# A recurrence whose small matrix products stand in two groups a step instead of three

## The chip, the core and the metric

The kernel runs on one core of a Trainium2 chip. The core has five engines with a queue of their own each: TensorE (PE in the profile, with its weight loads as PEld), VectorE (DVE), ScalarE (ACT), GpSimd (POOL) and SyncE (SP), which only issues transfers here. An engine takes its queue in order; an instruction that waits for a semaphore holds up what is queued behind it. Matrix products read SBUF and write PSUM. The metric is the time of one execution on the device, in microseconds.

## The reference

Two transformer layers in float32. The first layer, which the change touches, adds three things: its input, a gated feed-forward (hidden 512, inner 1408) and a "TTT" attention, in which a small weight matrix is trained while the sequence is read. Batch 4, 512 tokens, 32 heads of width 16, in 32 steps of 16 tokens:

```python
def step(carry, x):
    W1_s, b1_s = carry
    xq, xk, xv, eta_mb = x
    Z1 = xk @ W1_s + b1_s
    grad = _ln_fused_l2_bwd(Z1, xv - xk, ln_w, ln_b)
    Attn1 = jnp.tril(xq @ xk.swapaxes(-1, -2))
    b1_bar = b1_s - jnp.tril(eta_mb) @ grad
    Z1_bar = xq @ W1_s - eta_mb * Attn1 @ grad + b1_bar
    W1_new = W1_s - (last_eta * xk).swapaxes(-1, -2) @ grad
    b1_new = b1_s - jnp.sum(last_eta * grad, axis=-2, keepdims=True)
    out = xq + _ln(Z1_bar, ln_w, ln_b)
    return ((W1_new, b1_new), out)
```

The outputs are normalised over 512 and projected. The second layer (latent attention and a group of experts) follows and is not changed.

## The kernel before, in words

Everything is in one function, `trunk_kernel`, that records instructions for all engines. The recording layer then puts each engine's instructions in an order of its own: an instruction whose data are early can be placed ahead of earlier ones. An instruction that is handed to `tc.keep_in_program_order` is held in the program's order on its engine. The resulting order of each engine is fixed when the program is built; it can be read from the built program ("the built order").

**The recurrence** (loop at L781) has 32 steps, n = 0 to 31. A state of 128 (b, head) blocks lives in the PSUM tile wacc. A step has these parts:

- `weights_out` (L328): the state is copied from wacc into the block-diagonal operand wq_bd (L332: two copies on DVE, two on ACT) and, masked for two heads, into wh (L335, ACT).
- `first_product` (L338): one full product with bones, and 16 **quarter products** pz (128 rows by 32 columns of the array, so that four stand side by side): keys times state, and keys times queries, from sk and wq_bd.
- `queries_out` (L410): 16 quarter products, queries times state, from wh and wq_bd into the PSUM tile pso (the *query product*).
- `gradient` (L353): a chain of small operations, nearly all on DVE (L356 to L390), to grad.
- `out_operands` (L418): grad is masked for two heads into gh on POOL (L421) and the attention part of pz into a_bd on DVE (L424).
- `update` (L393): four copies of grad into the block-diagonal g_bd (L395, DVE and ACT), then 16 quarter products from km and g_bd into wacc (the *update*), and gsum on DVE.
- `emit_out` (L434): 16 quarter products from gh and a_bd into pso, on top of the query product (the *output product*); then DVE adds the bias into zch (L449) and updates bias_o (L450). After the fourth step of a chunk, POOL stores zch to DRAM (z, L454) and loads it back in another layout (zb, L456).
- `prepare` (L303) for the next step, on POOL: the load of kv (L307), sk (L314), four copies of the queries into the other columns of wq_bd (L316), km (L321).

**The work beside it.** The feed-forward, the projections and the finishing of earlier chunks (`finish`, L545: squares pn_sq, a full product with bones, reciprocals, and more) are generators, each of whose pieces carries a cost in microseconds; `fill(us)` (L702) records pieces until their costs add up to what is due. The step calls it three times with the entries of GAPS, 11, 3 and 8 us (10, 3 and 7 in the last chunk): between output operands and update, between update and output product, and behind the output product. Their products are full ones (128 rows by 128 columns), 256 or 512 columns long: pf (gate and up), pd (down), pj (projections, transposes, finishing). A float32 product shows as two passes in the trace. The loads of their weights (wg, wu, wd) are issued by SP.

All quarter products are recorded through one helper, `mm` (L116, L117), so they all carry line L117 in the profile and are told apart by their tiles.

Of the kernel before, what the change touches and what calls it, by code (L numbers as in the profile page):

```python
# [23 lines left out]
NH, HD, K = 32, 16, 16  # L24
NM = L // K
# [30 lines left out]
def trunk_kernel(ctx: ExitStack, tc: tile.TileContext, a: dict, out: bass.AP):  # L56
    nc = tc.nc
# [48 lines left out]
    with ExitStack() as px:  # L106
# [7 lines left out]
        quarters = [slice(32 * q, 32 * q + 32) for q in range(4)]  # L114

        def mm(out, lhsT, rhs, start=True, stop=True):  # L116
            nc.tensor.matmul(out, lhsT=lhsT, rhs=rhs, start=start, stop=stop, skip_group_check=True)  # L117

        def psum():
            return ps_pj.tile([P, 512], F32, tag="pj", name="pj")  # L120
# [48 lines left out]
        def by_head(name):  # L169

            return a[name].rearrange("(al r) (be bp h d) -> al r be bp h d", al=4, be=4, bp=2, h=2)[:, 0, :, 0]
# [4 lines left out]
        for name in ("gamma", "beta"):  # L176
            nc.scalar.dma_start(
                out=row[name].rearrange("o (be al x) -> o be al x", be=NC, al=4),
# [13 lines left out]
        def spread_row(dst, src):  # L192
            pr = psum()[:, : src.shape[-1]]
            mm(pr, one_row, src)
            nc.vector.tensor_copy(dst, pr)
# [10 lines left out]
        for h in range(2):  # L206
            r = slice(4 * h, 4 * h + 4)
            nc.gpsimd.dma_start(
                out=sel8[r], in_=a["bones"].rearrange("(be h r) p -> h be r p", be=4, h=2)[h, :, 0]
# [32 lines left out]
        def features(ch, w, got, tag, bufs):  # L242

            t = got[ch] = wk.tile([P, NC, CW], F32, tag=tag, name=f"{tag}_{ch}", bufs=bufs)
            for be in range(NC):
                pp = psum()[:, :CW]
                for c in range(NC):
                    mm(pp, w[:, c, be * P : (be + 1) * P], xTs[ch][:, c, :], c == 0, c == NC - 1)
                nc.scalar.copy(t[:, be, :], pp)
                yield 1.72  # L250
# [49 lines left out]
        def spread(ap):  # L300
            return ap.unsqueeze(2).to_broadcast([P, NG, HD])
# [26 lines left out]
        def weights_out(n):  # L328

            flat = wacc.rearrange("p b be d -> p (b be) d")  # L330
            for al, r in enumerate(quarters):
                (nc.vector.tensor_copy if al < 2 else nc.scalar.copy)(wq_bd[r, :, al, :HD], flat[r])  # L332
            wh = wk.tile([P, NG, 2, HD], F32, tag="wh", name=f"wh_{n}")
            for h in range(2):
                nc.scalar.mul(wh[:, :, h, :], flat, m2[:, h : h + 1])  # L335
            return wh.rearrange("p g h d -> p g (h d)")

        def first_product(n, pre):  # L338

            pz = ps_st.tile([P, NG, 2 * HD], F32, tag="pz", name=f"pz_{n}")  # L340
            mm(pz[:, :, :HD], bones, gsum.rearrange("p b al d -> p (b al) d"), True, False)
            for b in range(B):
                for be, r in enumerate(quarters):
                    mm(
                        pz[r, 4 * b : 4 * b + 4, :],
                        pre["sk"][:, 4 * b + be, :],
                        wq_bd[:, 4 * b + be],
                        False,
                        True,
                    )  # L350
            return pz
# [41 lines left out]
        def update(n, g, pre):  # L393
            for be, r in enumerate(quarters):
                (nc.vector.tensor_copy if be < 2 else nc.scalar.copy)(g_bd[r, :, be, :], g[r])  # L395
            for b in range(B):
                for al, r in enumerate(quarters):
                    mm(
                        wacc[r, b].rearrange("p be d -> p (be d)"),
                        pre["km"][:, 4 * b + al, :],  # L400
                        g_bd[:, 4 * b + al].rearrange("p be d -> p (be d)"),
                        False,
                        True,
                    )
            flat = gsum.rearrange("p b al d -> p (b al) d")
            nc.vector.scalar_tensor_tensor(flat, g, ntok, flat, ALU.mult, ALU.add)
# [3 lines left out]
        def queries_out(n, wh):  # L410

            po = ps_st.tile([P, NC, 4, K + 1], F32, tag="pso", name=f"pso_{n}")
            for be in range(NC):
                for b, r in enumerate(quarters):
                    mm(po[r, be, :, :K], wh[:, 4 * b + be, :], wq_bd[:, 4 * b + be, :, HD:], be == 0, False)
            return po

        def out_operands(n, g, pz):  # L418
            gh = wk.tile([P, NG, 2, HD], F32, tag="gh", name=f"gh_{n}")
            for h in range(2):  # L420
                nc.gpsimd.tensor_scalar_mul(gh[:, :, h, :], g, m2[:, h : h + 1])  # L421

            for be, r in enumerate(quarters):
                nc.vector.scalar_tensor_tensor(  # L424
                    a_bd[r, :, be, :K],
                    pz[r, :, HD:],
                    1.0,
                    mneg[r].unsqueeze(1).to_broadcast([32, NG, K]),
                    ALU.add,
                    ALU.mult,  # L430
                )
            return gh

        def emit_out(n, po, gh):  # L434

            ch, i = divmod(n, CH)
            for al in range(4):
                for b, r in enumerate(quarters):
                    mm(
                        po[r, :, al, :],  # L440
                        gh[:, 4 * b + al].rearrange("p h d -> p (h d)"),
                        a_bd[:, 4 * b + al],
                        False,
                        True,
                    )
            if i == 0:
                zch[ch] = wk.tile([P, NG, CT], F32, tag="zch", name=f"zch_{ch}", bufs=1)
            flat = po.rearrange("p be al t -> p (be al) t")
            nc.vector.tensor_add(zch[ch][:, :, i * K : (i + 1) * K], flat[:, :, :K], spread(bias_o))  # L449
            nc.vector.tensor_add(bias_o, bias_o, flat[:, :, K])  # L450
            if i == CH - 1:
                dst = z_d[ch].rearrange("(x hd) b t -> hd x b t", hd=32)
                for b, r in enumerate(quarters):
                    nc.gpsimd.dma_start(out=dst[:, :, b, :], in_=zch[ch][r])  # L454
                zbs[ch] = wk.tile([P, NC, CW], F32, tag="zb", name=f"zb_{ch}", bufs=1)
                nc.gpsimd.dma_start(out=zbs[ch], in_=z_d[ch].rearrange("(be p) b t -> p be (b t)", p=P))  # L456
# [45 lines left out]
        for j, name in enumerate(("gamma", "beta")):  # L502
            nc.gpsimd.dma_start(
                out=ch8[4 * j : 4 * j + 4], in_=by_head(name).rearrange("al be h d -> be al (h d)")
# [197 lines left out]
        def fill(us):  # L702
            nonlocal due
            due += us
            while due > 0 and (v := next(work, None)) is not None:
                due -= v
# [39 lines left out]
        def zeroed(name, shape):  # L746
            t = one.tile(shape, F32, tag=name, name=name)
            nc.gpsimd.memset(t, 0.0)
            return t


        wq_bd = zeroed("wq_bd", [P, NG, 4, 2 * HD])
# [28 lines left out]
        for n in range(NM):  # L781
            wh = weights_out(n)
            pz = first_product(n, pre)
            po = queries_out(n, wh)
            g = gradient(n, pz, pre)
            gh = out_operands(n, g, pz)

            gaps = GAPS if n // CH + 1 < NCHUNK else LAST_GAPS
            fill(gaps[0])
            update(n, g, pre)  # L790
            fill(gaps[1])
            emit_out(n, po, gh)
            fill(gaps[2])
            if n + 1 < NM:
                while (n + 1) // CH not in done:
                    fill(1.0)
                pre = prepare(n + 1)
# [111 lines left out]
    with ExitStack() as px:  # L909
# [197 lines left out]
        for e in range(E):  # L1107
            if e == 1:
# [9 lines left out]
                for t, rows in ((cos, slice(0, HALF)), (sin, slice(HALF, RD))):  # L1118
                    for k in range(E):
                        nc.sync.dma_start(  # L1120
                            out=t[:HALF].rearrange("p (k e j) -> p k e j", k=NCHUNK, e=E)[:, :, k],
# [10 lines left out]
            if e == 2:  # L1132

                pb = psp.tile([P, 2, E, NHG], F32, tag="pa", name="pb")
                for j, wr in enumerate((wkr, wqr)):
                    by_head = b_raw[:, j].rearrange("p (hg h) -> p h hg", h=HPG)
                    for m in range(E):
                        t = ident[:, m:RD:2] if m < 2 else wr[:, HALF * (m - 2) : HALF * (m - 1)]
                        for h, r in enumerate(quarters):
                            nc.tensor.matmul(  # L1140
                                pb[r, j, m],
                                lhsT=t,
                                rhs=by_head[:, h],
                                start=True,
                                stop=True,
                                skip_group_check=True,
# [18 lines left out]
    with ExitStack() as px:  # L1165
# [227 lines left out]
        for u, (hg, b) in enumerate(units):  # L1393
# [15 lines left out]
            for i in range(E):  # L1409
                n = E * u + i  # L1410
# [121 lines left out]
```

## Time and profile before

| | |
|---|---|
| three runs | 2002.38, 2007.29, 2008.54 us; median 2007.29 |
| profiled execution | 2001.78 us, span 2000.0 us |
| the 32 steps | 47.3 us (first product of step 0) to 903 us |
| PE busy / POOL busy | 1939.4 us / 515.9 us |
| 128x32 quarter products, 16 a step of each kind | pz 0.276 us a pass, query 0.219, update 0.222, output 0.225 (their lengths overlap) |

The busy share of an engine is that of its instructions' modelled lengths. Quarter products are issued so that they overlap, so distances between starts say more than lengths. A wait ("idle before ... <- releaser") is the time in which an engine did nothing, put down to what released it. PEclk is the share of its full clock that TensorE was granted.

### The profile page before, as it was taken

To read this page: it belongs to the slowest core of one execution; us is meant where nothing else is said; L and a number is where in the kernel's file an instruction comes from. 1 tells how busy PE (TensorE), PEld (TensorE's weight loads), DVE (VectorE), ACT (ScalarE), POOL (GpSimd) and SP (SyncE) were. 2 spreads that over 40 slices of the span, in tenths; PEclk is the share of its full clock that TensorE was granted. 3 is DMA by queue.
4 is the path that set the end of the run, shared out by engine and by line. 5 is a ranking of instruction groups with operands and counts; after the bars stand their busy time and mean duration, and the time that the engine had idled before them with its cause. 6 is when DMAs were issued, how large, how long until landed. Compare 5 with 4: busy or idle time off the path is not lost.

```text
span 2000.0 us, 32373 instructions
## 1 busy us (share of the span) xinstructions
PE 1939.4 (97%) x11626; PEld 1233.0 (62%) x11626; DVE 1170.9 (59%) x2579; ACT 815.8 (41%) x1695; POOL 515.9 (26%) x619
## 2 busy tenths in 40 slices
PE   8999999999999999998999999999999999999997
PEld 6777676767767676743777745555555555555555
DVE  5445757475666566574555566555655556555664
ACT  2224334334334342432222165554554455445552
POOL 4334343424243343412000101111211121322110
PEclk9999999999999999999999999999999999999999
DMA  6657566646465455746652144444444434333343
GB/s 167 199 138 212 143 188 169 181 115 192 123 172 167 124 175 152 229 117 200 224 167 63 44 112 127 123 102 109 105 103 107 106 102 112 93 97 97 102 107 103
DMA packets 227307, 273.50 MB, mean 137 GB/s; under 512 B 88587, under 2 KB 117452, under 8 KB 226508
## 3 DMA queue, kind: packets, MB, share of 16 engines
q1 hardware_dynamic: 206656, 239.28, 43.5%
q0 software_dynamic: 8992, 26.84, 4.7%
q10 hardware_dynamic: 11500, 5.32, 0.9%
q8 instruction: 93, 1.52, 0.3%
q14 instruction: 66, 0.54, 0.1%
HBM read 174.18 MB, written 34.87 MB: 105 GB/s over the span
## 4 chain that ended last, share of the span: by engine, by line
PE 49%; DVE 1%; DMA 1%; SPq 0%; ACT 0%; issue 0%; DVEq 0%; ACTq 0%
PE pc L1254 11%; PE sc L1207 9%; PE pq L1184 8%; PE px L1301 5%; PE p L1301 4%; PE pk L1184 3%; PE epg L976 3%; PE epo L1039 1%; PE epu L976 1%; PE eox L1069 1%; PE pvo L891 1%; PE pw L866 1%; PE eo L1069 1%; DMA gu<-in_gu 0%; SPq L1246 0%
## 5 line engine op out<-in xcount | busy, mean ns | idle before, releaser
L1225 DVE TENSOR_REDUCE st<-sc 128x1 f32<-128x512 f32 x256 | 168.9, 681 | 242.4 <-PE sc L1207 242.4
L1227 ACT ACTIVATE prob<-sc,st 128x512 f32<-128x512 f32 x256 | 175.1, 686 | 213.7 <-DVE st L1225 213.5
L1254 PE MATMUL pc<-prT,lv 128*128 128x512 f32 x512 | 232.5, 597 | 5.2 <-DMA out<-y 3.9
L1236 DVE STREAM_TRANSPOSE tt<-prob 128x512 f32<-128x512 f32 x256 | 178.4, 700 | 46.6 <-ACT prob L1232 37.1
L1232 ACT ACTIVATE prob<-prob,st 128x512 f32<-128x512 f32 x256 | 182.0, 720 | 58.2 <-DVE st L1231 58.2
L117 PE MATMUL pf<-xT,wg 128*128 128x256 f32 x704 | 174.7, 390 | 4.1 <-DMA wg<-in_wg 2.7
L1184 PE MATMUL pq<-cq,uq 128*128 128x512 f32 x384 | 175.2, 592 | 0.0
L117 PE MATMUL pf<-xT,wu 128*128 128x256 f32 x704 | 168.2, 382 | 0.9 <-DMA wu<-in_wu 0.7
L117 PE MATMUL pd<-wd,hid 128*128 128x512 f32 x352 | 166.3, 601 | 1.3 <-DMA wd<-in_wd 1.3
L1254 PEld LDWEIGHTS pc<-prT,lv 128*128 128x128 f32 x512 | 96.8, 191 | 106.8 <-issue 104.5
L117 PEld LDWEIGHTS pf<-xT,wg 128*128 128x128 f32 x704 | 133.1, 193 | 31.2 <-issue 4.9
L1207 PE MATMUL sc<-k,q 32*128 32x512 f32 x1024 | 145.7, 617 | 2.5 <-ACT prob L1227 2.5
L117 PEld LDWEIGHTS pf<-xT,wu 128*128 128x128 f32 x704 | 134.7, 192 | 20.7 <-DMA wu<-in_wu 2.1
L478 DVE SCALAR_TENSOR_TENSOR hid<-pf,us,sg 128x256 f32<-128x256 f32 x88 | 42.0, 478 | 155.3 <-ACT sg L477 154.9
L1184 PEld LDWEIGHTS pq<-cq,uq 128*128 128x128 f32 x384 | 74.1, 193 | 90.7 <-issue 89.7
L314 POOL TENSOR_SCALAR sk<-k,m 128x256 f32<-128x256 f32 x64 | 60.3, 952 | 180.9 <-PE pz L117 168.7
L1195 POOL TENSOR_TENSOR kr<-kr,t2k 128x512 f32<-128x512 f32 x16 | 20.3, 1268 | 332.3 <-DVE t2k L1194 332.3
L421 POOL TENSOR_SCALAR gh<-grad,m 128x256 f32<-128x256 f32 x64 | 61.9, 976 | 153.2 <-DVE grad L390 131.0
L117 PEld LDWEIGHTS pd<-wd,hid 128*128 128x128 f32 x352 | 63.3, 190 | 60.4 <-issue 44.2
L1207 PEld LDWEIGHTS sc<-k,q 32*128 32x128 f32 x1024 | 48.4, 185 | 82.8 <-issue 73.2
L477 ACT ACTIVATE sg<-pf,gs 128x256 f32<-128x256 f32 x88 | 41.6, 473 | 134.8 <-PE pf L117 134.5
L1256 ACT COPY ctxT<-pc 128x512 f32<-128x512 f32 x64 | 37.4, 584 | 132.0 <-PE pc L1254 132.0
(316 smaller groups left out, 3455.2 us busy)
## 6 DMA issues: line engine op xcount, KB each, us to landing
prT<-tt SPq DMA_DIRECT2D x1016, 64.0 KB, 2.0
wd<-in_wd SPq DMA_DIRECT2D x176, 256.0 KB, 3.1
wg<-in_wg SPq DMA_DIRECT2D x88, 256.0 KB, 3.1
wu<-in_wu SPq DMA_DIRECT2D x88, 256.0 KB, 3.0
cq<-lat_d SPq DMA_DIRECT2D x48, 256.0 KB, 3.8
rows<-rows SPq DMA_DIRECT2D x128, 66.0 KB, 2.2
kv<-rows POOLq DMA_DIRECT2D x32, 264.0 KB, 4.3
gu<-in_gu SPq DMA_DIRECT2D x3, 2048.0 KB
```

Source lines behind the costliest of these rows:

```text
L117: nc.tensor.matmul(out, lhsT=lhsT, rhs=rhs, start=start, stop=stop, skip_group_check=True)
L314: nc.gpsimd.tensor_scalar_mul(sk[:, :, :, h, :], at(k1[ch], slice(0, P)), m2[:, h : h + 1])
L421: nc.gpsimd.tensor_scalar_mul(gh[:, :, h, :], g, m2[:, h : h + 1])
L976: nc.tensor.matmul(ps, lhsT=w[:, c, :], rhs=x[:, c], start=start and c == 0, stop=c == 1, skip_group_check=True)
L1184: nc.tensor.matmul(ps, lhsT=columns(ws[hg][w]), rhs=x, start=(i == 0), stop=(i == len(srcs) - 1))
L1207: nc.tensor.matmul(ps[h], lhsT=qk[f"q{c}"][r, i * P : (i + 1) * P], rhs=qk[f"k{c}"][r, :], start=(n == 0), stop=(n == 2),)
L1225: pin(nc.vector.tensor_reduce(mx, ps[h], AX.X, ALU.max, negate=True))
L1227: pin(nc.scalar.activation(pr, ps[h], AF.Exp, bias=mx, scale=1.0, accum_out=sm))
L1232: pin(nc.scalar.mul(pr, pr, sm))
L1236: nc.vector.transpose(out=tt[:, :, h - 2], in_=pr.rearrange("p (k kq j) -> p kq k j", kq=4, j=32))
L1254: pin(nc.tensor.matmul(pc, lhsT=lv[:, b, k, :], rhs=at[:, :, k, :], start=(k == 0), stop=(k == E - 1)))
L1301: nc.tensor.matmul(ps[:, q, :], lhsT=a[:, k, q * P : (q + 1) * P], rhs=w[:, k, :], start=start and k == 0 and q == 0, stop=k == 1, skip_gr ...
```

## The change

`mm` returns the instruction. The output product of step n-1 is recorded behind the first product of step n, so it runs one gap later; the last one stays behind its own step. The query product of step n is recorded behind the update of step n. The first product of each column position is held in the program's order: four of the query product's 16 and four of the output product's. Nothing else differs: no operation is added or taken away, and the gaps keep their costs.

```diff
         def mm(out, lhsT, rhs, start=True, stop=True):
-            nc.tensor.matmul(out, lhsT=lhsT, rhs=rhs, start=start, stop=stop, skip_group_check=True)
+            return nc.tensor.matmul(out, lhsT=lhsT, rhs=rhs, start=start, stop=stop, skip_group_check=True)
...
             for be in range(NC):
                 for b, r in enumerate(quarters):
-                    mm(po[r, be, :, :K], wh[:, 4 * b + be, :], wq_bd[:, 4 * b + be, :, HD:], be == 0, False)
+                    ins = mm(po[r, be, :, :K], wh[:, 4 * b + be, :], wq_bd[:, 4 * b + be, :, HD:], be == 0, False)
+                    if be == 0:
+                        tc.keep_in_program_order(ins)
             return po
...
             for al in range(4):
                 for b, r in enumerate(quarters):
-                    mm(
+                    ins = mm(
                         po[r, :, al, :],
                         gh[:, 4 * b + al].rearrange("p h d -> p (h d)"),
                         a_bd[:, 4 * b + al],
                         False,
                         True,
                     )
+                    if al == 0 and n + 1 < NM:
+                        tc.keep_in_program_order(ins)
...
             wh = weights_out(n)
             pz = first_product(n, pre)
-            po = queries_out(n, wh)
+            if n:
+                emit_out(n - 1, po, gh)
             g = gradient(n, pz, pre)
             gh = out_operands(n, g, pz)
 
             gaps = GAPS if n // CH + 1 < NCHUNK else LAST_GAPS
             fill(gaps[0])
             update(n, g, pre)
+            po = queries_out(n, wh)
             fill(gaps[1])
-            emit_out(n, po, gh)
+            if n + 1 == NM:
+                emit_out(n, po, gh)
             fill(gaps[2])
```

## The prediction

> **What bounds the kernel now.** I read the page first. TensorE (PE) is busy for 97% of the span, and the chain that ended last is made of PE work nearly alone: 49% of the span lies on PE and at most 1% on any other engine. So a microsecond taken from PE is a microsecond of time, and an engine beside it matters only where PE waits for it. The steps (0 to 31) run from 47 us (first product of step 0) to 905 us (the last output product).
>
> ```profile
> PE 1939.4 (97%) x11626; PEld 1233.0 (62%) x11626; DVE 1170.9 (59%) x2579; ACT 815.8 (41%) x1695; POOL 515.9 (26%) x619
> ...
> PE 49%; DVE 1%; DMA 1%; SPq 0%; ACT 0%; issue 0%; DVEq 0%; ACTq 0%
> ```
>
> Second, the timeline of PE in one step (start, length, line, names, count of passes; a product is two passes). Every end is modelled, so I use the distance of starts.
>
> ```profile
> 302.10 1.89 PE L117 MATMUL pf<-xT,wu 128*128 128x256 f32 x8
> 303.83 1.04 PE L144 MATMUL pj<-ident,xt 128*128 128x128 f32 x8
> ...
> 308.14 0.59 PE L117 MATMUL pz<-gsum,bones 128*128 128x256 f32 x2
> 308.66 1.08 PE L117 MATMUL pz<-wq_bd,sk 128*32 128x128 f32 x32
> ...
> 324.70 0.65 PE L117 MATMUL wacc<-g_bd,km 128*32 128x64 f32 x32
> 325.17 0.66 PE L117 MATMUL pso<-a_bd,gh 128*32 128x68 f32 x32
> 325.76 3.72 PE L117 MATMUL pj<-xT,wk 128*128 128x256 f32 x16
> ```
>
> The reader is to see what a border costs. Four full products of 256 columns take 303.83-302.10 = 1.73 us, 0.43 each; the same product ahead of quarter products takes 308.66-308.14 = 0.52. Entering costs 0.09. Sixteen quarter products take 325.17-324.70 = 0.47 when quarter products follow and 325.76-325.17 = 0.59 when a full product does. Leaving costs 0.12, so one run of quarter products costs 0.21 over its work.
>
> Third, PE's waits from 40 to 910 us (total, times, longest).
>
> ```profile
> PE pso L117 <- POOL gh L421: 5.8, 4, 2.7
> PE pj L117 <- ACT pn_sq L549: 4.0, 2, 3.1
> PE wacc L117 <- ACT g_bd L395: 3.5, 4, 1.6
> PE pf L117 <- DMA wg<-in_wg: 2.7, 3, 2.0
> PE pz L117 <- ACT wq_bd L332: 2.5, 2, 1.4
> ...
> PE wacc L117 <- DVE g_bd L395: 1.8, 2, 1.3
> ...
> PE pso L117 <- DVE bias_o L450: 1.0, 1, 1.0
> ```
>
> These few microseconds are what a new order can win or lose besides the borders.
>
> **Part 1: the borders.** In the built order of PE I count runs of quarter products between full ones: 94 before, 71 after. Before, 28 runs hold first product and query product, 23 the output product alone, 21 the update alone; after, 30 hold update and query product, 27 first product and the previous output product. 23 runs fewer at 0.21 us: **-4.8 us**. No product is added or removed. Of the price, 0.18 (by the query product's exit, 0.56 against 0.47) to 0.21 is shown.
>
> **Part 2: waits that go.** The output product now runs a whole gap behind its gh on POOL: the 5.8 goes. The query product no longer waits for bias_o: 1.0. The finishing of a chunk of rows is placed elsewhere by the new order; before, two of its products (L549) waited 4.0. One wait for wg, 2.0 of the 2.7, stood behind the update of step 3, which will now be late itself. The waits for g_bd (5.3) and wq_bd (2.5) are worked out anew below. Two of the waits were followed by a slow clock:
>
> ```profile
> 712.50:716.00 3.50, 3.21 (x39) 2.62 (x40) 1.98 (x5) 1.72 (x5) 3.37 (x5) 0.71 0.74 193
> ...
> 816.80:820.00 3.20, 3.16 (x6) 1.92 (x7) 3.00 (x7) 0.00 (x0) 2.54 (x4) 0.53 0.75 227
> ```
>
> These are rows by stretch; the third figure from the right (0.71, 0.53) is the granted clock. With 0.82 in the 4.0 us after the first it lost 0.29x3.5+0.18x4.0 = 1.7 us there, and 0.47x3.2 = 1.5 us in the second. Total of what was lost before: 5.8+1.0+4.0+2.0+5.3+2.5+3.2 = 23.8 us.
>
> **Part 3: waits for the gradient, after.** The update needs all of g_bd. From first product to g_bd is a serial run of VectorE (DVE):
>
> ```profile
> 147.73 0.42 DVE L356 TENSOR_REDUCE s<-pz 128x16 f32<-128x256 f32 x1 [9.64 <-PE pz L117]
> ...
> 156.22 0.90 DVE L395 COPY g_bd<-grad 32x256 f32<-32x256 f32 x2
> ```
>
> 9.4 us in step 3. The change puts the two additions behind the output product (zch 0.42, bias_o 0.17) into this run: +0.6 in every step. PE covers it with the full products that the built order leaves between first product and update, and with 0.6 of quarter products. So a step waits for DVE work minus cover minus about 0.4. (Tried on the steps before, this is right within 1 us: step 10 gives 1.8, the trace 1.4; step 24 gives 1.0, the trace 1.5.) With the built order of DVE and PE, sums from the rows' durations, DVE against cover: step 3, 9.9 against 3.5; step 7, 9.4 against 8.6; step 10, 12.3 against 10.6; step 14, 11.8 against 9.7; step 18, 10.5 against 9.5; step 22, 12.1 against 10.6; step 23, 11.1 against 9.7; step 25, 14.3 against 13.8; steps 17 and 21, 18.5 and 20.0 against 16.4 and 18.5, where the old order had the same sums and waited little, so 0.5 each. The others are covered. Sum: 6.0+0.4+1.3+1.7+0.6+1.1+1.0+0.1+0.5+0.5 = 13.2.
>
> **Step 3** is nearly half of that. The built order puts the update's first product behind two groups of full products (3.5 us) and the other fifteen behind two more pairs; PE takes its queue in order, so it stands until g_bd, some 6 us, with 6.9 us of ready work behind it. Bounds 5.0 to 6.5. A slow clock follows: 1.5 to 3.6 (the stretch from 48 to 100 us, with a wait of 2.5 at 50, had 0.93 of 52.0 us); I take 2.0, near the two in the steps. Five other waits worked out here last 1.6 to 2.9. Before, five in the steps were that long (2.0 for wg, 2.7 and 1.5 for gh, 1.7 for g_bd, 3.1 for the finishing) and two brought a slow clock; the new ones are shorter, so I count one, 1.7 (bounds 0 to 5).
>
> The Trainium skill ("TensorE: Matmul & The Clock Gate", Why this matters for your kernels) warns of idle gaps above some 3 us, after which the clock falls back to half. Here the waits of 1.7 us (at 712) and 3.1 us (at 816) brought it, one of 2.8 us at 264 did not. By the page step 3 alone would pay, an estimated 1.7 us by its window of 3413 ns, and the sum would be 2.0 better; if every wait over 1.5 us paid as at 712, all five would, and it would be 6.8 worse.
>
> **Part 4: what the move delays.** The query product reads the queries in wq_bd, so POOL's four copies of the next step's queries (L316, 1.7 us) now wait until behind the update instead of running during the gradient. Queued behind them on POOL are sk, km, gh, row sums and the DMA issues of kv, z and zb. The next first product waits for the copies; cover is the full products between update and first product. In the built order it is over 5 us in most steps, but 0.9 (step 7), 1.1 (step 17), 1.7, 2.6, 3.5 and 3.9 in six. Step 7: gh ends 2.0 behind the gradient, two kv issues 1.2, copies 1.7, so 4.9; PE is there at 3.4: wait 1.6. Step 17: gh 2.0, km 1.8, copies 1.7 against 3.6: 2.0. The rest 0.3. Sum 3.9 (bounds 1 to 8).
>
> The output rows of a chunk are complete one gap later, and so are z, zb and the finishing. For chunk 0 the zb load is queued behind the copies for step 5 and km of step 6. From the start of update 4: update and query product 1.2, copies 1.7, km 1.8, kv issue 0.6, zb's median landing 5.5, squares 1.1, in all 11.9; PE asks at 1.1+6.9+1.3 = 9.3, amid step 5's first product: 2.6 and latencies, 2.9 (bounds 1 to 4). For chunk 1 zb is behind gh of step 8. From its first product: DVE 9.9, gh 2.0, row sum 1.3, issues 1.4, landing 5.5, squares 1.1, in all 21.2, against 17.3+1.5 = 18.8 on PE: 2.4 (0 to 3). Chunks 2 to 6 have cover. One later finishing product in step 5, whose DVE run now holds four reciprocals of 1.75: 1.0 (0 to 3). Sum 6.3.
>
> **Sum.** Lost after: 13.2+2.0+1.7+3.9+6.3 = 27.1, against 23.8 before: +3.3; with the borders **-1.5 us**. The profiled execution took 2001.78 us (span 2000.0); the median of the three runs is 2007.29, 5.5 above it, and I take the difference over: 2007.3-1.5 = **2005.8**. A measurement of this kernel can tell some 0.3%, 6 us, from no change.
>
> **Rivals.** *Waits at their low ends* (0.20): step 3 5.0, its clock 1.5, other gradient waits 4, copies 1, finishing 2: 13.5 against 23.8, so -10.3-4.8 = -15; halfway to the forecast, -8: 1999. For it: the old order's longest waits stand where the new one has cover. Against: the wait in step 3 is fixed by the order.
>
> *The borders are not saved* (0.18): what is lost is lost between any two kinds of quarter products, not at the full ones. For it: the query product starts 0.09 after the first product's last pass, where passes of a kind follow at 0.01. Against: update to output product shows 0.47. Then +3.3: 2010.6.
>
> *POOL takes the bound* (0.19), the slower end: the copies behind the update, in the six steps with under 4 us of cover. If another pair (1.8) or a row sum with its load (1.3 and more) is ahead of them each time, each waits 2.5, 15 in all in place of 3.9: -1.5+11.1 = +9.6: 2016.9. It decides from a mean wait of 0.9 (no gain); from 1.9 it is slower by over 0.3%. For it: POOL waits 36.9 us for the query product in these copies already. Against: POOL is 26% busy.
>
> **How the numbers follow.** Forecast 0.43, its own range 1999 to 2012 (two in ten of it under -6, a twentieth over +6). Faster: 0.09+0.20 = 0.29; slower: 0.02+0.19 = 0.21; within 0.3%: 0.50. The range reaches to both outer cases: 1995 to 2017.
>
> **What would show it.** Right: PE's wait for gh gone; a wait of some 6 us for g_bd in step 3 with a slow clock behind it; first products of steps 8 and 18 waiting for POOL's copies; update and query product starting 0.47 apart. Wrong: no wait in step 3, or zb and the copies late in most chunks.

## The result and the profile after

The changed kernel takes **2013.72 us** (median of 9 runs, 2008.71 to 2016.23) against 2006.96 for the kernel before on the same chip (9 runs, 2002.38 to 2011.06): a ratio of **1.0033**, 95% interval 1.002 to 1.0045. Forecast was 1.5 us less; it is some 7 us more, inside the range and on the other side of no change.

The engines' line and the chain of the changed kernel's page (span 2012.2 us, 2013.97 us in all):

```profile
PE 1939.8 (96%) x11626; PEld 1236.3 (61%) x11626; DVE 1161.4 (58%) x2579; ACT 815.6 (41%) x1695; POOL 511.4 (25%) x619
...
PE 49%; DVE 1%; DMA 1%; SPq 0%; ACT 0%; issue 0%; DVEq 0%; ACTq 0%
```

Work and chain are as before: the page does not say where the time is lost. PE's waits between 40 and 910 us do (total, times, longest):

```profile
PE pf L117 <- DVE hid L482: 8.5, 5, 2.3
PE wacc L117 <- ACT g_bd L395: 8.5, 4, 6.0
PE pz L117 <- POOL wq_bd L316: 6.3, 4, 4.6
PE pj L117 <- ACT pn_sq L553: 4.2, 2, 3.7
PE pj L117 <- DVE pn_sq L546: 3.1, 5, 1.1
...
PE pf L117 <- DMA wg<-in_wg: 1.8, 1, 1.8
```

The reader is to see that the waits for gh (5.8 us) and bias_o (1.0) are gone, as meant, and that each of the first three rows here is larger than any row of the old list.

**An account of the steps.** From the first product of step 0 to the last output product the two profiled executions take 855.4 and 860.7 us. For each pair of neighbouring products I take the usual distance of their starts (borders included) as work, and what is over it by more than 0.15 us as lost; a slow clock counts as lost. Before: 813.5 work, 41.9 lost. After: 807.8 work, 52.9 lost. So the work fell by 5.7 us and the losses rose by 11.0 (the split hangs on what is taken as usual, by some 2 us; the sum of the two does not). This sum explains +5.3 of the pair's +12.2 us; the rest lies behind the steps (a finishing that waits 4.2 us at 930 us with half clock behind it, where it waited 2.9 before: +3.9 by the last pj product; further on, slow-clock stretches of 6.8 instead of 3.4 us in code that the change doesn't touch). The profiled execution of before was also 5.2 us under its median, so the pair exaggerates; sizes below are judged by ratios of many runs.

Two stretches of the changed kernel's PE timeline show single losses. Step 3, where the first update product stands early:

```profile
157.09 0.42 PE L117 MATMUL wacc<-g_bd,km 128*32 128x64 f32 x2 [5.95 <-ACT g_bd L395]
157.44 3.69 PE L117 MATMUL pf<-xT,wg 128*128 128x256 f32 x8
```

Step 5, where a finishing product waits in the middle of the first product:

```profile
203.63 3.78 PE L117 MATMUL pj<-pn_sq,bones 128*128 128x512 f32 x4 [3.73 <-ACT pn_sq L553]
207.34 0.43 PE L117 MATMUL pz<-wq_bd,sk 128*32 128x128 f32 x3
```

And the granted clock behind the first of them, behind the second, and behind the longest wait for POOL's wq_bd, at 840 us (third figure from the right):

```profile
157.00:161.00 4.00, 3.91 (x11) 3.09 (x12) 0.44 (x1) 0.03 (x1) 1.23 (x2) 0.51 0.10 37
203.60:208.00 4.40, 4.37 (x24) 1.83 (x26) 0.00 (x0) 1.96 (x2) 0.00 (x0) 0.50 0.12 19
840.00:844.00 4.00, 3.90 (x68) 3.52 (x69) 2.72 (x8) 2.38 (x6) 1.82 (x3) 0.57 0.69 180
```

Eight passes of pf take 3.69 us here and 1.89 elsewhere: the slow clock behind the wait of step 3 cost 0.49x4.0 = 2.0 us, the one in step 5 0.50x4.4 = 2.2 us and the one at 840 us 0.43x4.0 = 1.7 us.

### The profile page after: what moved, and what is told of

Same layout as the page of the kernel before. It is cut to its first block, busy times and chain, and to the rows that moved or that the text cites. A ratio compares the mean times of both kernels' runs of the same rounds, so it can differ in the third digit from the quotient of the medians.

```text
span 2012.2 us, 32353 instructions
## 1 busy us (share of the span) xinstructions
PE 1939.8 (96%) x11626; PEld 1236.3 (61%) x11626; DVE 1161.4 (58%) x2579; ACT 815.6 (41%) x1695; POOL 511.4 (25%) x619
## 4 chain that ended last, share of the span: by engine, by line
PE 49%; DVE 1%; DMA 1%; SPq 0%; ACT 0%; issue 0%; DVEq 0%; ACTq 0%
PE pc L1261 11%; PE sc L1214 9%; PE pq L1191 8%; PE px L1308 5%; PE p L1308 4%; PE pk L1191 3%; PE epg L983 3%; PE epo L1046 1%; PE epu L983 1%; PE eox L1076 1%; PE pvo L898 1%; PE pw L873 1%; PE eo L1076 1%; DMA gu<-in_gu 0%; SPq L1253 0%
## 5 line engine op out<-in xcount | busy, mean ns | idle before, releaser
L117 PE MATMUL pf<-xT,wg 128*128 128x256 f32 x704 | 174.6, 389 | 10.4 <-DVE hid L482 8.5
L117 PEld LDWEIGHTS pd<-wd,hid 128*128 128x128 f32 x352 | 63.4, 190 | 60.8 <-issue 41.9
```

The source lines that it names most:

```text
L117: return nc.tensor.matmul(out, lhsT=lhsT, rhs=rhs, start=start, stop=stop, skip_group_check=True)
```

## The experiments

**Theories.** A: the borders are saved as worked out, and more than that is lost to new waits: step 3's update; and at the ends of chunks, where rows, z and zb are one gap late. B: a wait that is removed is replaced by the next late thing. C: POOL's copies behind the update are the loss. Of the borders, the rival says that they cost nothing by themselves. Each ratio is to the kernel before on the same chip. Not all kernels ran on the same chip, so compare the ratios and not the medians; the interval of a difference of two of them is some ±0.002, 4 us.

| kernel | median us | ratio, 95% interval | runs of quarter products |
|---|---|---|---|
| changed kernel | 2013.72 | 1.0033 (1.0020 to 1.0045) | 71 |
| the same, second time | 2013.46 | 1.0039 (1.0023 to 1.0054) | 71 |
| 1 update held in order | 2005.73 | 1.0014 (0.9999 to 1.0029) | 69 |
| 2 query product alone moved | 2000.46 | 0.9989 (0.9974 to 1.0004) | 92 |
| 3 extra border | 2023.81 | 1.0096 (1.0072 to 1.0121) | 103 |
| 4 its control | 2020.05 | 1.0082 (1.0063 to 1.0101) | 70 |
| 5 update held, chunk's last output product in its step | 2001.54 | **0.9976 (0.9963 to 0.9989)** | 75 |
| 6 as 5, zch and bias_o behind g_bd | 2002.25 | 0.9992 (0.9977 to 1.0006) | 81 |
| 7 as 1, zch written twice | 2008.99 | 1.0019 (1.0003 to 1.0035) | 68 |
| 8 output product moved at chunk ends only | 2011.28 | 1.0034 (1.0019 to 1.0049) | 86 |
| 9 as 5, update not held | 2007.46 | 1.0012 (1.0002 to 1.0023) | 77 |

A profile shows one execution, and some are far from their kernel's median: those of kernels 1, 7 and 9 are the slowest of their runs (2014.43, 2014.84, 2014.02 us), that of kernel 3 the fastest (2014.41). The changed kernel's two (2013.97, 2014.71) are close to it. So the waits below say which ones there are; what a change is worth is read from the ratios.

The changed kernel, run again beside kernels 5 to 7, was expected so:

> The changed kernel itself, as it is, beside the three kernels that follow on the same chip: 1.0033 of the kernel before, between 1.002 and 1.0045.

It came out at 1.0039, which is the same.

**1. The update held in order.** In `update`:

```diff
-                    mm(
+                    ins = mm(
                         wacc[r, b].rearrange("p be d -> p (be d)"),
...
+                    if b == 0:
+                        tc.keep_in_program_order(ins)
```

> The changed kernel, with the first four products of each update held in program order as well. In the order of TensorE the first update product of step 3 then stands behind 10.4 us of full products instead of 3.5, like the other fifteen; the runs of quarter products are 69 (71 in the changed kernel), and the other steps keep their cover within 0.9 us. Theory A (the loss is the wait of step 3 with its clock, 6.0 + 2.0 us, and several smaller ones): 8 us under the changed kernel, some 2006, between 2003 and 2008. Rival B (a wait removed there is only moved to the next thing that is late): within 2 us of the changed kernel, 2012 to 2015. Rival C (the loss is POOL's copies behind the update): they are untouched, so as B.

Measured: 1.0014, 2005.7 us: 4 to 5 us under the changed kernel by the ratios, whose intervals overlap (kernel 9 tests the same again). The wait of 6.0 us in step 3 is gone; a wait of 1.8 us for wg stands in its place, as it did before the change (2.0). Step 3 and its clock are a real part of the loss, smaller than the 8 us by what is late next. The other rows stay (hid 9.8, POOL's wq_bd 6.8, pn_sq 4.8 and 3.5 us).

**2. The query product alone moved.** The output product is back in its own step, its first four products still held in order. In the loop:

```diff
-            if n:
-                emit_out(n - 1, po, gh)
...
             fill(gaps[1])
-            if n + 1 == NM:
-                emit_out(n, po, gh)
+            emit_out(n, po, gh)
```

> The changed kernel, with the output product put back into its own step (behind the gap after the update), so that only the query product is moved, behind the update. Runs of quarter products: 92 (94 before, 71 changed); the update has its cover in step 3, the output rows and z are as early as before, zch and bias_o lie behind the gradient as before. Theory A (no border is saved, the wait for gh stays at about 5.8 us, and of the new losses only POOL's copies remain, 6.3 us against 2.5 before): 3 us over the kernel before, some 2010, between 2007 and 2012; waits for the query copies of POOL (L316) between 4 and 8 us, none for hid over 2 us in sum. Rival C (POOL's copies are the whole loss and grow further): 2013 or more. Rival D (the copies have cover; they were late in the changed kernel only because z and zb came late on POOL's queue): within 1 us of the kernel before.

Measured: 0.9989, 2000.5 us: neither theory A's 2010 nor C's 2013, but below even rival D (the copies have cover; within 1 us of before, which the interval allows). PE's waits:

```profile
PE pf L117 <- DMA wg<-in_wg: 7.6, 6, 2.6
PE wacc L117 <- ACT g_bd L395: 5.4, 3, 2.2
...
PE pz L117 <- POOL wq_bd L316: 2.6, 1, 2.6
PE pf L117 <- DVE hid L482: 1.8, 1, 1.8
```

POOL's copies stand behind the update in every step here, and PE waits for them once. So the copies are not late by themselves, and the whole loss of the changed kernel comes with the move of the output product and the order that it brings (step 3 has its cover here). My theory A was wrong in this part: the gh wait went too (0.2 us left), as this order has more full products between update and output product.

**3 and 4. The price of a border.** One full product of one column in each step, in the middle of the output product (3) or beside the full product ahead of the first product (4):

```diff
             for al in range(4):
+                if al == 2:
+                    tc.keep_in_program_order(mm(po[:, 0, 0, :1], bones, zcol, False, False))
```

```diff
             mm(pz[:, :, :HD], bones, gsum.rearrange("p b al d -> p (b al) d"), True, False)
+            mm(pz[:, 0, :1], bones, zcol, False, False)
```

In 3 the third group of the output product is held in order as well.

> The changed kernel with one more product in each of the 32 steps: a full one of one column, of weights that are there by a column of zeros, so that the values stay. It stands in the middle of the output product, between its second and third group of four, and so splits a run of quarter products in two: 103 runs. Compared with the next kernel, which has the same extra product at the full product ahead of the first product (70 runs): 33 runs more at 0.21 us, 6.9 us longer (between 5 and 8) if the price of a border read from the trace is right (theory A); within 1.5 us of it if what is lost is lost between any two kinds of products and a border costs nothing by itself (rival: the borders are not saved).

> The changed kernel with the same extra full product of one column in each step, here next to the full product that opens the first product, where it splits no run: 70 runs, as in the changed kernel (71). Both theories: longer than the changed kernel by the product itself, 32 times at most 0.1 us, some 2 to 4 us: 2014 to 2018. It is the control of the kernel with the product in the middle.

Measured: 2023.81 and 2020.05 us, 3.8 apart (2.8 by the ratios, whose intervals overlap). PE's timeline of 3, and then of 4, in the same step:

```profile
489.14 0.42 PE L117 MATMUL pso<-a_bd,gh 128*32 128x68 f32 x16
489.49 0.38 PE L117 MATMUL pso<-zcol,bones 128*128 128x1 f32 x2
489.80 0.45 PE L117 MATMUL pso<-a_bd,gh 128*32 128x68 f32 x16
490.17 1.99 PE L117 MATMUL pf<-xT,wg 128*128 128x256 f32 x8
```

```profile
495.57 0.66 PE L117 MATMUL pso<-a_bd,gh 128*32 128x68 f32 x32
496.16 1.99 PE L117 MATMUL pf<-xT,wg 128*128 128x256 f32 x8
```

From the first output product to the next full product it is 1.03 us against 0.59. The extra product costs PE 0.44 there and 0.11 to 0.12 in the control (pz starts 0.64 behind bones instead of 0.52): a split costs some 0.33 on PE, 32 of them 10.5 us. That is the price of a border on PE, and it is there.

What of it reaches the end these runs do not tell. The difference of the two ratios, 0.0014, has an interval of some ±0.003: from 3 us less to 9 us more, which holds theory A's 6.9 as well as the rival's 0 to 1.5. And the control missed its forecast: it is 9 to 10 us over the changed kernel by the ratios, not 2 to 4, for a product that costs PE 32x0.12 = 3.8 us. Kernel 3 is 11 to 13 us over the changed kernel, near the 32x0.44 = 14.1 us that its product costs PE. The two profiles can't decide it either, since they stand the other way round than the medians (2014.41 us for 3, 2021.89 for 4). In them the account of the steps gives 820.3 work and 45.2 lost for 3, 810.8 work and 58.1 lost for 4, with shorter waits in 3 (hid 5.6 us against 9.1, wq_bd 5.6 against 8.2, g_bd 8.1 against 9.8). That shorter waits take up part of a border's price is one reading of this pair; it is not shown.

**5. The chunk's last output product left in its own step**, with the update held as in 1; that output product is no longer held in order, the other three of a chunk are:

```diff
-            if n:
+            if n % CH:
                 emit_out(n - 1, po, gh)
...
-            if n + 1 == NM:
+            if n % CH == CH - 1:
                 emit_out(n, po, gh)
```

> The update pinned as in the kernel that held the update in order, and of each chunk's four output products the last one left in its own step; only the other three are put behind the next first product. Runs of quarter products: 75. The rows of a chunk, z, its load zb and the finishing are then as early as before the change, and in the steps behind a chunk's end (4, 8, 12 and so on) VectorE's gradient run is without zch and bias_o. Theory A (rows a gap late are the larger part of the loss): the 3.9 us and the 1.9 of slow clock at the finishing in step 5 go, the 4.65 us for POOL's query copies at 840 us goes (they stood behind zb), and the waits for hid, 8 to 10 us, fall by half; six more borders cost 1.3: some 10 us under the kernel with the update pinned, 1997, faster than before by 0.2 to 0.6%. Rival B (each wait that goes is replaced by the next): 2003 to 2008. Rival C (POOL's copies are late by themselves): the wait for wq_bd of POOL stays over 4 us.

Measured: 0.9976, 2001.5 us: faster than both kernels, 7 to 8 us under kernel 1 by ratio, where 10 were expected; B and C are out. PE's waits:

```profile
PE pj L117 <- ACT pn_sq L555: 5.3, 3, 3.5
PE pf L117 <- DMA wg<-in_wg: 4.2, 3, 3.0
...
PE pf L117 <- DVE hid L484: 2.9, 2, 1.6
...
PE pz L117 <- POOL wq_bd L316: 1.3, 2, 0.8
```

The row for hid fell from 9.8 to 2.9 and the one for wq_bd from 6.8 to 1.3 (8.5 and 8.1, 6.3 and 5.3 in the changed kernel's two profiles).

**6 and 7. Is it the 0.6 us of zch and bias_o in the gradient run?** In 6 they are taken out of `emit_out` into a function of their own, `out_rows`, and recorded behind the update's copies (as in 5 where a chunk ends), and zch is held there; in 7 zch is written twice:

```diff
             update(n, g, pre)
+            if n % CH:
+                out_rows(n - 1, po)
```

```diff
             nc.vector.tensor_add(zch[ch][:, :, i * K : (i + 1) * K], flat[:, :, :K], spread(bias_o))
+            nc.vector.tensor_add(zch[ch][:, :, i * K : (i + 1) * K], flat[:, :, :K], spread(bias_o))
```

> The kernel before this one, with zch and bias_o of the other three steps recorded behind the copies of g_bd and held there, so that they lie behind the gradient run and not in it. 81 runs of quarter products. If the 0.6 us in the gradient run are what makes hid and g_bd late (theory A): the two waits together 2 to 4 us shorter, six borders 1.3 dearer, so 1 to 3 us less than the kernel before this one. If hid is late because of its place in VectorE's order alone (rival): no gain, and 1 us more for the borders.

> The kernel with the update pinned, with zch written twice, the second time with the same values: 0.42 us more of VectorE work in each gradient run, nothing else added; 68 runs of quarter products. Theory A (the two additions in the run delay hid and g_bd one for one where there is no cover, about nine steps): 3 to 5 us over the kernel with the update pinned. Rival (VectorE is 58% busy and takes it up): within 1 us.

Measured: 6 is 0.9992, some 3 us over kernel 5, not under it (hid 5.0 us against 2.9). 7 is 1.0019 against 1.0014 in kernel 1: 1 us, and the intervals overlap widely; its hid row is 7.3 us where kernel 1 has 9.8. Neither supports the 0.6 us; but 6 split six of the update's groups from their query products, and in both the built order moved other pieces too, so small effects stay hidden. That these two additions delay hid one for one is not supported: hid's row is not shorter without them in 6 nor longer with more of them in 7. The time of 7 alone would allow theory A's 3 to 5 us.

**8. Only the chunk ends moved.** The query product behind the update everywhere, the output product behind the next first product, and held in order, only where a chunk ends:

```diff
-            if n:
+            if n and n % CH == 0:
                 emit_out(n - 1, po, gh)
...
-            if n + 1 == NM:
+            if n % CH < CH - 1 or n + 1 == NM:
                 emit_out(n, po, gh)
```

> The query product behind the update in every step, but the output product is put behind the next first product only at the end of each chunk (in 7 of the 31 steps); the other 24 stay in their own step. 86 runs of quarter products; the update of step 3 has its full cover (10.4 us) without a hold. It is the kernel with the query product alone moved, plus the part that makes the rows of a chunk, z, zb and the finishing one gap late. Theory A (this part is most of the loss): the waits of the changed kernel at the chunks' starts are there again, pn_sq in step 5 with its clock (3.9 + 1.9), POOL's query copies behind zb in step 29 (3 to 4.6), hid behind the gradient run in steps 8 to 24 (5 to 8 in sum): 1.0035 of the kernel before, between 1.002 and 1.005, some 9 us over the kernel with the query product alone moved. Rival (the loss is step 3 and the output products within the chunks): within 3 us of the query product alone, 0.998 to 1.0005 of the kernel before.

Measured: 1.0034, 2011.3 us: as theory A said, 9 us (0.0045±0.002) over kernel 2 (0.9989), by moving 7 output products; the one other difference is that kernel 2 holds the output product in order in the other 24 steps too. PE's waits:

```profile
PE pf L117 <- DVE hid L482: 9.7, 5, 2.5
PE pz L117 <- issue: 6.4, 1, 6.4
...
PE pj L117 <- ACT pn_sq L553: 3.3, 2, 1.7
```

Of theory A's waits, hid's and the one in step 29 are there and longer than forecast; the finishing in step 5 waits 1.7 us instead of 3.9, with no slow clock behind it. The second row is the first product of step 29. The profile found no releaser; ScalarE's timeline in the same kernel shows one:

```profile
839.93 1.06 ACT L553 ACTIVATE pn_sq<-zb 128x1024 f32<-128x1024 f32 x1 [13.05 <-DMA zb<-z]
841.00 0.74 ACT L332 COPY wq_bd<-wacc 32x256 f32<-32x256 f32 x2
```

ScalarE has stood 13 us for zb, and the copies of the state that the first product needs are queued behind the squares of zb. PE starts at 841.84.

**9. Kernel 5 without the hold on the update.**

> The kernel with the chunks' last output product left in its own step, without the hold on the update: the update's first product of step 3 stands again behind 3.5 us of full products, and step 7 has 7.3 us of cover for 9.9 of VectorE work. 77 runs. Theory A (step 3 costs 6 us and its clock): 5 to 9 us over the same kernel with the update held, 1.0005 of the kernel before, between 0.999 and 1.0025. Rival (the wait of step 3 is given back by later waits): within 2 us of it, 0.9965 to 0.9985.

Measured: 1.0012 against 0.9976, 2007.5 us against 2001.5: 6 to 7 us for step 3 (wait 5.9 us at 159.0), within theory A's 5 to 9. With 1 it closes a square: update held or free, by chunk ends late or in place, gives 1.0014 and 1.0033 to 1.0039 (late), 0.9976 and 1.0012 (in place). Each of the two costs 4 to 8 us; together they cost 11 to 13, a little less than the 15 of the two taken singly from kernel 5.

## Why the prediction was wrong

**Borders, -4.8: right on PE.** Work on PE fell by 5.7 us for 23 runs, between the first product of step 0 and the last output product (at 903 us before the change, not at 905). Whether such a sum arrives whole at the end kernels 3 and 4 leave open.

**Waits that go: right.** gh, bias_o and the wait for wg in step 3 are gone from the trace.

**Step 3, 6.0 and its clock 2.0: right to the tenth** (5.95 and 2.0). Its price at the end is 4 to 7 us (kernels 1 and 9), and with the wait away PE waits for wg instead (1.8 us in kernel 1, 3.0 in kernel 5).

**The other gradient waits, 7.2: too high.** They are 3.1 (9.1 for g_bd in all, less 6.0). Step 18 waits 1.8, the rest under 0.6 each.

**One other slow clock, 1.7: too low.** There were two, 2.2 us behind the finishing in step 5 and 1.7 at 840 us in step 29, both behind waits that the next two items bring.

**POOL's copies, 3.9: too high for the steps that it priced, and the wrong item.** Step 8 waits 0.9 (1.6 forecast), step 18 0.5 (2.0), step 24 0.3. The row's 6.3 us holds 4.6 in step 29, which stood among "the rest 0.3". POOL and ScalarE in the changed kernel, in two views:

```profile
831.40 0.76 POOL L460 DMA_DIRECT2D zb<-z  x1 [2.69 <-DMA z<-zch]
834.18 1.82 POOL L321 TENSOR_SCALAR km<-kv,m2n 128x256 f32<-128x256 f32 x2 [2.03 <-DMA kv<-rows]
835.96 0.58 POOL L307 DMA_DIRECT2D kv<-rows  x1
836.58 1.82 POOL L321 TENSOR_SCALAR km<-kv,m2n 128x256 f32<-128x256 f32 x2
838.36 1.69 POOL L316 COPY wq_bd<-q 32x256 f32<-32x256 f32 x4
```

```profile
838.01 1.06 ACT L553 ACTIVATE pn_sq<-zb 128x1024 f32<-128x1024 f32 x1 [10.73 <-DMA zb<-z]
839.08 0.74 ACT L332 COPY wq_bd<-wacc 32x256 f32<-32x256 f32 x2
```

The wait is put down to POOL, which ended last, at 840.05; ScalarE ended at 839.82. Both stood behind the late pair: POOL's issue of zb waits 2.7 us for z (and its km 2.0 more for a kv load), and ScalarE's squares wait 10.7 for zb. Before the change the squares of the same chunk ran a step earlier, without a wait, some 12 us ahead of these copies:

```profile
815.74 1.05 ACT L549 ACTIVATE pn_sq<-zb 128x1024 f32<-128x1024 f32 x1
```

The query product's place had little to do with it: in kernel 2, where it is the same, step 29 has no such wait.

**Finishing, 6.3: about right as a sum** (7.3 for pn_sq in its two rows; step 5 waits 3.7, forecast 2.9, but step 8 only 0.5, forecast 2.4).

**The step that failed** is the sentence in part 4, "Chunks 2 to 6 have cover", and what it stands for: I priced late rows by the finishing products alone, and not by what is queued behind z and zb on POOL and ScalarE, nor by what the new place of z does to the built order of VectorE. Kernel 8 isolates it, but for the hold: 9 us from moving seven output products. Leaving them in place takes 7 to 8 us off kernel 1 (kernel 5) and 4 to 5 off the changed kernel (kernel 9). In the trace two rows carry it. One is step 29 above. The other is hid, 1.4 us before and **8.5** after, in steps 8, 12, 16, 20 and 24, and no term of the sum had it. VectorE in step 16 of the changed kernel:

```profile
497.58 0.42 DVE L390 TENSOR_TENSOR grad<-u,rl 128x256 f32<-128x256 f32 x1
498.04 0.77 DVE L395 COPY g_bd<-grad 32x256 f32<-32x256 f32 x2
498.82 0.48 DVE L406 SCALAR_TENSOR_TENSOR gsum<-grad,ntok,gsum 128x256 f32<-128x256 f32 x1
499.34 0.88 DVE L482 SCALAR_TENSOR_TENSOR hid<-pf,us,sg 128x256 f32<-128x256 f32 x2
```

and in kernel 5:

```profile
485.14 0.43 DVE L374 TENSOR_TENSOR pair<-xh,by_tok 128x256 f32<-128x256 f32 x1
486.82 0.48 DVE L484 SCALAR_TENSOR_TENSOR hid<-pf,us,sg 128x256 f32<-128x256 f32 x1 [1.24 <-ACT sg L483]
489.00 0.48 DVE L484 SCALAR_TENSOR_TENSOR hid<-pf,us,sg 128x256 f32<-128x256 f32 x1 [1.69 <-ACT sg L483]
489.40 0.17 DVE L367 TENSOR_TENSOR rl<-r,kv 128x16 f32<-128x16 f32 x1
```

hid empties the PSUM tile pf, of which there are two. In the changed kernel both hid stand behind the whole gradient run, and PE, two gate products ahead, waits 2.3 us for a tile. In kernel 5, as before the change, two hid stand in the middle of the run, ahead of rl, which needs kv. The built order of POOL differs in the same way at that place: z, then the kv loads of the next steps (before, kernel 5); two or three kv loads, then z (kernel 8, changed kernel). That the order of kv and z is what moves hid in the built order was not tried by itself; it fits all four kernels.

**The sum again, with what was measured:** against the forecast of the losses, hid +7.1 (8.5-1.4), POOL's row +2.4, slow clocks +2.2 (5.9 against 3.7), the wg wait that is left +1.8, finishing +1.0, gradient -4.1: +10.4, where the forecast rise of 3.3 and the measured one of 11.0 differ by 7.7. The rows of waits and the account by distances are two measures; the 2.7 us between them are not resolved.

**The rivals.** "The borders are not saved" is refuted on PE by kernels 3 and 4, and open at the end. Its evidence was a misreading: the passes of the first product start in fours, 7 ns apart, with 0.09 us from one four to the next, so the 0.09 ahead of the query product is the usual distance. "POOL takes the bound" gave a time not far off (2016.9) by a mechanism that did not act: kernel 2 has all of POOL's copies late and is the second fastest.

**The clock.** The 6.0 us wait of step 3 was followed by half clock (0.51 over 4.0 us). The page "TensorE: Matmul & The Clock Gate" of the Trainium skill (Why this matters for your kernels) ties a fall of the clock to idle gaps above some 3 us, and this wait agrees. For shorter ones the length does not decide here: the same 2.3 us wait for hid in step 16 was followed by a clock of 0.64 in kernel 1 and of 1.00 in the changed kernel, and by 0.65 (500 to 504 us) in the changed kernel's own second profile:

```profile
500.00:504.00 4.00, 4.00 (x13) 3.24 (x13) 0.04 (x1) 0.47 (x1) 2.56 (x4) 0.64 0.56 175
```

```profile
499.80:503.80 4.00, 3.92 (x18) 3.48 (x19) 0.42 (x2) 0.16 (x1) 3.21 (x5) 1.00 0.95 276
```

## What to carry to other kernels

When a step is moved later, price what is queued behind its transfers and their readers on every engine that takes its queue in order, and read the built order for unrelated instructions that change places; here that was worth more than the borders which the move saved. Split such a change by position before judging it: the same move did no harm in three steps of four and lost 4 to 9 us in the fourth, and one product placed early in one step cost 4 to 7. A wait that is removed need not come back whole: step 3 lost 8 us in the trace, and with its wait away another stood close behind.

## What the runs showed that was not expected

- Splitting a run of quarter products by a one-column full product costs PE some 0.33 us, more than the 0.21 of an entry and an exit read beside long full products.
- The control product, which costs PE 3.8 us in sum, made the kernel 9 to 10 us slower; no run here shows why.
- A wait of 2.3 us at the same place of the same kernel was followed by a granted clock of 0.65 in one run and 1.00 in another.
- The wait in step 29 is put down to POOL in one kernel and to nothing ("issue") in another, with ScalarE's queue behind zb in both.
